# Quarters of the former unit's output product among the seven products of gate and up

## The chip, the cores and the metric

The kernel runs on one core of one Trainium2 chip. A core has five engines that run side by side: TensorE (PE in the profile; its weight loads have a row of their own, PEld), VectorE (DVE), ScalarE (ACT), GpSimd (POOL) and SyncE (SP, which issues most DMAs). The metric is the device time of one execution in microseconds (us). The time before is 747.75 us, the median of three runs (747.67, 747.75 and 748.01).

## The reference

Two transformer layers on x of shape 4 x 256 x 256 in float32, each with an attention of 16 heads and an FFN of 1024 hidden units, all with a layer norm ahead and a residual behind. The part that matters here is the FFN of the second layer:

```
up_gate = jnp.einsum('bsd,hd->bsh', x, W1)
up_lin = jnp.einsum('bsd,hd->bsh', x, W3)
hidden = jax.nn.silu(up_gate) * up_lin
hidden = fwht(hidden)
out = jnp.einsum('bsh,dh->bsd', hidden, W2)
```

## The kernel before

The kernel runs first attention, first FFN, second attention and second FFN in that order. The second FFN (`ffn1`) works in eight units, n = 0 to 7: unit n is one batch of 256 tokens (b = n // 2) and one half of the 1024 hidden units (half = n % 2). A unit has two parts.

The first part is `gated1`: the gate and up products of this batch with this half. Each is computed by a scheme with seven block products in place of eight (a Winograd form of Strassen's), written in `seven_products`. The seven run on TensorE in the order 5, 1, 2, 6, 3, 7, 4. Each product is four float32 matmuls of 128x128 by 128x128; the trace shows a float32 matmul as two records, so a product is eight records. The products go into three PSUM buffers, x (`gu_x`), y (`gu_y`) and z (`gu_z`). Product 5 goes to y; 1 to x; 2 to z; 6 is added to x; 3 is added to y; 7 is added to x; 4 is added to x. Because a sum is built up in a buffer from which partial values are taken, there are waits between the products:

- Product 6 may add to x only when ScalarE has copied x as product 1 left it (line 638).
- Product 7 may add to x only when ScalarE has copied x as product 6 left it (line 644).
- Product 4 may add to x only when VectorE has read x as product 7 left it (line 650, which forms the block c22 of the result).

Behind product 4, ScalarE copies x once more (line 653), then takes the silu of the gate half (line 852), and VectorE multiplies by the up half (line 853). The result is the tile h, the hidden values of the unit. In the last unit, n = 7, silu and multiplication are done in two halves of 128 tokens each, and the first half needs only products 5, 1, 2, 6 and 3.

The second part is `down`: the output product of unit n - 1. For each of two blocks of 128 tokens (t = 0, 1) it issues four float32 matmuls of 128x128 by 128x256 into a PSUM bank `po_f` (line 590). A batch's two units add up in the same two banks, and behind the second of them VectorE adds the residual (line 597) and SyncE stores 128 KB of output (line 600). The Walsh-Hadamard transform has been folded into the weights `w2h` before. A quarter of `down` is two float32 matmuls, four records; there are 16 records in all.

Two things set the order of the work. The code's order is: all of `gated1` of unit n, some norms and block sums for later batches (`normed`, `left_of`), then all of `down` of unit n - 1. The framework then plans each engine's order: it goes through the instructions with its own estimate of each duration, gives each engine the earliest instruction in the code's order that is ready by that estimate, and passes over one that is not ready yet. The engine then runs the planned order as it stands and waits where the estimate was wrong. So `down` may already be taken between two products of `gated1`, though it stands behind them in the code.

The first FFN uses the same `down` on lines 530 and 536.

Of the kernel before, what the change touches and what calls it, by code (L numbers as in the profile page):

```python
# [48 lines left out]
def two_layers(ctx, tc, consts, tables, x, wq, wkv, wo, w_gate, w_up, w_down,  # L49
# [26 lines left out]
    def bank(shape, name):  # L76
        return ps1.tile([P, *shape], F32, tag="bank", name=name)

    def page(name):

        return work.tile([P, 4, T], F32, tag="page", name=name, bufs=8)
# [24 lines left out]
    def load_ffn(src, shape, name):  # L106
        t = fpool.tile([P, *shape], F32, tag="fw", name=name)
        nc.sync.dma_start(t, src)
        return t
# [20 lines left out]
    down_sb = load_ffn(w_down, (NF, D), "w_down")  # L130
# [388 lines left out]
    def ffn0():  # L519
        hs, xn = {}, dict(enumerate(xn_f))  # L520
        for n in range(8):
            b, gc = divmod(n, 2)
            hs[n] = h = gated(xn[b], gate_sb, up_sb, 4 * gc, "h")
            a = page("a")
            nc.scalar.activation(a, h, AF.Abs)
            keep_two_of_four(a, h)
            if gc == 0 and b + 2 < B:
                xn[b + 2] = normed(b + 2, by_dma=True)
            if n >= 2:
                down(hs, n - 2, down_sb)  # L530
            if n == 4:
                xn1[0] = normed(0, by_dma=True)
            if n == 6:
                xn1[1] = normed(1, by_dma=True)
                left1[0] = left_of(xn1[0])
        return lambda: [down(hs, n, down_sb) for n in (6, 7)]

    def gated(xnT, w_g, w_u, f0, name):

        ps = []  # L540
        for w in (w_g, w_u):
            o = wide("pgu").rearrange("p two (f t) -> p (two f) t", t=T)
            for j in range(4):
                for c in range(NC):
                    nc.tensor.matmul(  # L545
                        o[:, j, :], lhsT=w[:, c, f0 + j, :], rhs=xnT[:, c, :],
                        start=(c == 0), stop=(c == NC - 1),
                    )
            ps.append(o)
        s, h = page("s"), page(name)  # L550
        nc.scalar.activation(s, ps[0], AF.Silu)
        nc.vector.tensor_tensor(h, ps[1], s, ALU.mult)
        return h

    def keep_two_of_four(a, h):

        c = []
        counts = work.tile([P, 8, T], BF16, tag="page", name="counts", bufs=8)  # L560
        for i in range(3):
            n = 3 - i
            ci = counts[:, (0, 3, 5)[i] : (3, 5, 6)[i], :]
            nc.vector.tensor_tensor(
                ci, a[:, i : i + 1, :].to_broadcast([P, n, T]), a[:, i + 1 :, :], ALU.is_ge
            )
            c.append({i + 1 + k: ci[:, k, :] for k in range(n)})
        sums = (
            (c[0][1], ALU.add, c[0][2], ALU.add, c[0][3], 2.0, ALU.is_ge),
            (c[1][2], ALU.add, c[1][3], ALU.subtract, c[0][1], 1.0, ALU.is_ge),  # L570
            (c[2][3], ALU.subtract, c[0][2], ALU.subtract, c[1][2], 0.0, ALU.is_ge),
            (c[0][3], ALU.add, c[1][3], ALU.add, c[2][3], 1.0, ALU.is_le),
        )
        for j, (u, op0, v, op1, w, bound, keep) in enumerate(sums):
            n = counts[:, 6 + j % 2, :]
            nc.vector.tensor_tensor(n, u, v, op0)
            nc.vector.tensor_tensor(n, n, w, op1)
            nc.vector.scalar_tensor_tensor(h[:, j, :], n, bound, h[:, j, :], keep, ALU.mult)
# [3 lines left out]
    def down(hs, n, w, last=False):  # L582


        b, gc = divmod(n, 2)
        if gc == 0:
            pos[b] = [bank([D], "po_f") for _ in range(NT)]
        for t in range(NT):
            for j in range(4):
                nc.tensor.matmul(  # L590
                    pos[b][t], lhsT=hs[n][:, j, t * P : (t + 1) * P],
                    rhs=w[:, 4 * gc + j, :], start=(gc == 0 and j == 0),
                    stop=(gc == 1 and j == 3),
                )
            if gc == 1:
                x = xs[b * NT + t]
                nc.vector.tensor_tensor(x, pos[b][t], x, ALU.add)
                if last:
                    at = (b * NT + t) * P
                    nc.sync.dma_start(out[at : at + P, :], x)  # L600

# [6 lines left out]
    def left_of(xnT):  # L610

        s = late.tile([P, 4, P], F32, tag="xs4", name="xs4", bufs=4)
        x11, x12, x21, x22 = (xnT[:, c, t * P : (t + 1) * P] for t in range(2) for c in range(2))
        for i, a, b, op in (
            (0, x21, x22, ALU.add), (1, s[:, 0], x11, ALU.subtract),
            (2, x11, x21, ALU.subtract), (3, x12, s[:, 1], ALU.subtract),
        ):
            nc.vector.tensor_tensor(s[:, i], a, b, op)
        return x11, x12, s[:, 3], x22, s[:, 0], s[:, 1], s[:, 2]
# [10 lines left out]
    def seven_products(product, x, z, y, c11, c12, c21, c22, shape, z_alone=True):  # L630


        u = [late.tile(shape, F32, tag="u", name="u", bufs=4) for _ in range(3)]
        product(y, 5, True)
        nc.scalar.copy(u[1], y)
        yield
        product(x, 1, True)
        nc.scalar.copy(u[0], x)
        yield
        product(z, 2, z_alone)  # L640
        nc.vector.tensor_tensor(c11, z, u[0], ALU.add)
        yield
        product(x, 6, False)
        nc.scalar.copy(u[2], x)
        yield
        product(y, 3, False)
        nc.vector.tensor_tensor(c12, y, u[2], ALU.add)
        yield
        product(x, 7, False)
        last_of["sum"] = nc.vector.tensor_tensor(c22, x, u[1], ALU.add)  # L650
        yield
        product(x, 4, False)
        last_of["copy"] = nc.scalar.copy(c21, x)  # L653
        yield
# [99 lines left out]
    def st(shape, name):  # L754
        return st_pool.tile(shape, F32, tag="st", name=name)
# [74 lines left out]
                              [t[:, i, k] for k in range(4)]))  # L830
        return r

    def gated1(x, r, last):


        def product(o, i, first):
            for j in range(4):
                nc.tensor.matmul(  # L838
                    o[:, j, :], lhsT=r[j // 2][i - 1][:, j % 2, :], rhs=x[i - 1],
                    start=(first and j == 0), stop=True, skip_group_check=True,  # L840
                )

        gu = late.tile([P, 2, 4, T], F32, tag="qk", name="gu")
        c = gu.rearrange("p k (a m) (t c) -> p (k a) m t c", m=2, t=NT)
        for _ in seven_products(
            product, st([P, 4, P], "gu_x"), bank([4, P], "gu_z"), st([P, 4, P], "gu_y"),
            *(c[:, :, m, t, :] for t in range(2) for m in range(2)), [P, 4, P],
        ):
            pass
        s, h = page("s"), page("h1")  # L850
        for t in (slice(0, P), slice(P, T)) if last else (slice(0, T),):
            nc.scalar.activation(s[:, :, t], gu[:, 0, :, t], AF.Silu)
            nc.vector.tensor_tensor(h[:, :, t], gu[:, 1, :, t], s[:, :, t], ALU.mult)
        return h

    def ffn1():
        hs, left = {}, {0: left_of(xn_f[0])}
        for n in range(9):
            if n < 8:
                b, half = divmod(n, 2)  # L860
                hs[n] = gated1(left[b], r_ffn1[half], n == 7)
                if n == 0:
                    xn = {1: normed(1)}
                if half == 1 and b + 2 < B:
                    xn[b + 2] = normed(b + 2, by_dma=True)
                if half == 0 and b + 1 < B:
                    left[b + 1] = left_of(xn[b + 1])
            if n >= 1:
                down(hs, n - 1, w2h[0], last=True)

    xn_f, xn1, left1, w2h, r_ffn1 = [], {}, {}, [], []
    attention0()
# [8 lines left out]
    load_group1(1)  # L881

    finish_ffn0 = ffn0()
    xn_f.clear()
    ps2_open.close()
# [3 lines left out]
    st_open, st_pool = open_pool("st", bufs=4, space=PSUM)  # L889
    attention1(finish_ffn0)  # L890
    ffn1()
    st_open.close()

# [81 lines left out]
```

## Time and profile before

| what | value |
|---|---|
| median of three runs | 747.75 us |
| the profiled execution's own time | 746.65 us |
| its span in the profile | 744.8 us |
| PE busy over the span | 734.0 us, 99% |
| PEld busy over the span | 599.4 us, 80% |
| DVE, ACT, POOL busy | 464.3, 405.8, 338.2 us |
| second FFN, first product to last output sum | 660.75 to 741.91 us |
| units 3 to 6, from start of product 5 to the next unit's | 9.98 to 9.99 us each |

The span is the time between the first and the last instruction of the profiled execution; 1.85 us of that execution lie around it. Busy times of the engines add up to far more than the span, since they run side by side. In the timeline a row is a run of equal instructions: its start, its duration, the engine, the line, the tile written and the tiles read, and in square brackets how long the engine was idle before it and what ended that.

### The profile page before, as it was taken

Reading aid. Unit: us, or ns where it says so; the run is one execution under the profiler, and the core shown is the slowest. Engines: PE = TensorE matmul, PEld = TensorE weight load, DVE = VectorE, ACT = ScalarE, POOL = GpSimd, SP = SyncE. Lnnn points to the kernel's source line nnn. Section 1 sums busy time; section 2 is a strip of 40 time slices with the busy share of each in tenths; the row PEclk is TensorE's granted clock in tenths of the full one; section 3 lists DMA queues with packets and bytes.
Section 4 is the critical chain, followed back from the end, with each engine's and each line's share of the span. In section 5 each row is a group of like instructions: output and inputs, shape, how many; then the busy total and the mean of one; then the engine's idle time right before and its main releaser. Section 6 shows DMA issues by size and latency. Waiting matters only on the chain.

```text
span 744.8 us, 11648 instructions
## 1 busy us (share of the span) xinstructions
PE 734.0 (99%) x3956; PEld 599.4 (80%) x3956; DVE 464.3 (62%) x1398; ACT 405.8 (54%) x985; POOL 338.2 (45%) x479
## 2 busy tenths in 40 slices
PE   8999999999999999999999999999999999999998
PEld 5556566666667678888898999999998999899997
DVE  6999877888887517986655644464443548355333
ACT  2487887677767932322355555555554775324432
POOL 1587978887899801011125433343335683210000
PEclk9999999999999999999999999999999999999999
DMA  8732254434444451002224433542232222000000
GB/s 329 284 64 55 53 99 84 80 63 89 84 81 89 85 189 53 15 15 62 81 71 96 118 43 43 113 87 44 44 72 44 44 44 43 0 3 20 22 15 29
DMA packets 127882, 54.87 MB, mean 74 GB/s; under 512 B 121040, under 2 KB 123216, under 8 KB 127056
## 3 DMA queue, kind: packets, MB, share of 16 engines
q1 hardware_dynamic: 127824, 54.15, 31.5%
q8 instruction: 31, 0.51, 0.3%
q14 instruction: 27, 0.22, 0.1%
HBM read 22.94 MB, written 1.05 MB: 32 GB/s over the span
## 4 chain that ended last, share of the span: by engine, by line
PE 87%; DVE 8%; ACT 3%; POOL 1%; issue 1%; ACTq 0%; DVEq 0%; POOLq 0%
PE pj L440 11%; PE po L282 7%; PE pgu L545 7%; PE qk_x L764 7%; PE po_f L590 7%; PE po L294 6%; PE sc L205 6%; PE gu_x L838 4%; PE av L270 4%; PE qk_y L764 3%; PE v_x L770 3%; PE av L388 3%; PE sc L204 3%; PE v_zy L770 3%; PE gu_y L838 2%; PE av L273 2%
## 5 line engine op out<-in xcount | busy, mean ns | idle before, releaser
L225 POOL TENSOR_SCALAR p<-p,rs 128x128 f32<-128x128 f32 (+1 forms) x256 | 115.4, 469 | 149.6 <-DVE rs L222 146.4
L242 POOL TENSOR_SCALAR pl<-p 128x1536 uint16<-128x1536 uint16 x58 | 87.8, 1513 | 4.0
L207 DVE CUSTOM_DVE_ANT_0 p<-sc,cst 128x128 f32<-128x128 f32 (+1 forms) x256 | 79.8, 352 | 11.0 <-PE sc L205 8.3
L262 ACT COPY pT<-plT 128x1536 uint16<-128x1536 uint16 (+1 forms) x58 | 84.0, 1509 | 0.0
L217 ACT ACTIVATE p<-p,nb,r 128x128 f32<-128x128 f32 (+1 forms) x128 | 68.2, 534 | 18.7 <-DVE nb L214 18.6
L440 PE MATMUL pj<-wq,xnT 128*128 128x512 f32 x128 | 61.2, 595 | 1.8 <-DVE qT L503 1.1
L440 PE MATMUL pj<-wkv,xnT 128*128 128x512 f32 x128 | 60.3, 592 | 0.0
L217 ACT ACTIVATE p<-p,nb 128x128 f32<-128x128 f32 (+1 forms) x128 | 56.3, 445 | 5.7 <-DVE nb L212 5.7
L294 PE MATMUL po<-wo,zT 128*128 128x256 f32 x256 | 57.8, 379 | 0.0
L282 PE MATMUL po<-w_o,zT 128*128 128x256 f32 x256 | 57.7, 379 | 0.0
L155 POOL TENSOR_SCALAR ve<-mv 128x2 f32<-128x2 f32 x16 | 3.5, 219 | 116.0 <-DVE mv L152 115.6
L450 ACT ACTIVATE sq<-pj 128x512 f32<-128x512 f32 x64 | 31.0, 491 | 43.0 <-DVE qc L445 42.7
L294 PEld LDWEIGHTS po<-wo,zT 128*128 128x128 f32 x256 | 48.3, 190 | 7.0 <-ACT kT L514 0.6
L282 PEld LDWEIGHTS po<-w_o,zT 128*128 128x128 f32 x256 | 47.5, 190 | 5.8
L440 PEld LDWEIGHTS pj<-wkv,xnT 128*128 128x128 f32 x128 | 24.3, 190 | 30.2 <-issue 28.7
L445 DVE TENSOR_TENSOR qs<-pj,sin_s 128x512 f32<-128x512 f32 x64 | 35.4, 552 | 13.7 <-PE pj L440 13.2
L440 PEld LDWEIGHTS pj<-wq,xnT 128*128 128x128 f32 x128 | 23.5, 190 | 24.9 <-issue 19.8
L653 ACT COPY qk<-qk_x 128x512 f32<-128x512 f32 x16 | 9.4, 586 | 57.6 <-PE qk_x L764 57.6
L270 PE MATMUL av<-pT,v 128*128 128x256 f32 x128 | 38.8, 385 | 0.9 <-ACT pT L262 0.7
L205 PE MATMUL sc<-kT,qT 128*128 128x256 f32 x128 | 38.3, 381 | 0.0
L205 PE MATMUL sc<-qk 128*128 128x256 f32 x128 | 38.2, 380 | 0.0
L484 POOL TENSOR_TENSOR r<-ve,mhalf 128x12 f32<-128x12 f32 x16 | 37.3, 2328 | 0.8
(154 smaller groups left out, 1750.8 us busy)
## 6 DMA issues: line engine op xcount, KB each, us to landing
w<-in_w_dram SPq DMA_DIRECT2D x3, 1024.0 KB, 4.8
wq<-in_wq_dram SPq DMA_DIRECT2D x4, 512.0 KB, 7.4
wkv<-in_wkv_dram SPq DMA_DIRECT2D x4, 512.0 KB, 7.9
wo<-in_wo_dram SPq DMA_DIRECT2D x4, 512.0 KB, 10.2
w_qk<-in_w_q_dram SPq DMA_DIRECT2D x4, 512.0 KB, 4.6
w_qk<-in_w_k_dram SPq DMA_DIRECT2D x4, 512.0 KB, 5.5
w_v<-in_w_v_dram SPq DMA_DIRECT2D x4, 512.0 KB, 6.7
w_o<-in_w_o_dram SPq DMA_DIRECT2D x4, 512.0 KB, 6.5
```

The costliest lines, as they stand in the source:

```text
L205: nc.tensor.matmul(sc[:, P : 3 * P], lhsT=q[:, P:T], rhs=k, start=True, stop=True)
L207: last_of["mx"] = nc.vector.tensor_tensor_reduce(out=p[:, j, cols], in0=sc[:, cols], in1=mask[:, cols], scale=1.0, scalar=-3.0e38, op0=ALU ...
L217: last_of["exp"] = nc.scalar.activation(p[:, j, cols], p[:, j, cols], AF.Exp, bias=nb[:, j, i : i + 1], scale=SCALE1 if rq is None else rq ...
L225: nc.gpsimd.tensor_scalar(p[:, j, cols], p[:, j, cols], rs[:, j, i : i + 1], 1.0, ALU.mult, ALU.mult)
L242: last_of["planes"] = nc.gpsimd.tensor_scalar(o, i, 1.0, 1.0, ALU.mult, ALU.mult)
L262: copy(words.rearrange("p (n w) -> p w n", w=2), halves[:, :, js].rearrange("p w j n -> p w (j n)"),)
L270: nc.tensor.matmul(av, lhsT=v0, rhs=pT[:, 0:T], start=True, stop=False, skip_group_check=True)
L282: nc.tensor.matmul(po[:, t, :], lhsT=zT[:, j, t * P : (t + 1) * P], rhs=w[:, j, :], start=(t == j == 0), stop=(j == 3), skip_group_check=True,
L294: nc.tensor.matmul(po, lhsT=zTs[hd // 4][:, hd % 4, t * P : (t + 1) * P], rhs=w[:, hd, :], start=(hd == 0), stop=(hd == n - 1),)
L440: last_of[0] = nc.tensor.matmul(pj, lhsT=xnT[:, c, cols], rhs=w[:, g, c, :], start=(c == 0), stop=(c == NC - 1),)
L545: nc.tensor.matmul(o[:, j, :], lhsT=w[:, c, f0 + j, :], rhs=xnT[:, c, :], start=(c == 0), stop=(c == NC - 1),)
L764: last_of[1] = nc.tensor.matmul(o[:, j, :], lhsT=wqk[i - 1][:, j // 2, j % 2, :], rhs=x[i - 1], start=(first and j == 0), stop=True, skip_ ...
```

## The change

`down` becomes a generator that pauses four times, once behind each quarter (two float32 matmuls). `gated1` takes such a generator, `between`, and draws from it: one quarter behind product 6 (the fourth in order), and two quarters behind product 7 (the sixth in order), ahead of product 4. In `ffn1` the generator is `down` of unit n - 1, and what is left of it, the fourth quarter, is issued behind `gated1`, ahead of the norms and block sums that stood ahead of `down` before. Unit 0 has no former unit and gets an empty iterator. `down` of unit 7 is issued whole, as before. The first FFN runs its generators to the end at once, so that its order in the code stays.

```diff
+                if j == 1:
+                    yield
             if gc == 1:
                 x = xs[b * NT + t]
                 nc.vector.tensor_tensor(x, pos[b][t], x, ALU.add)
                 if last:
                     at = (b * NT + t) * P
                     nc.sync.dma_start(out[at : at + P, :], x)
+            yield
+
+    def run(*generators):
+        for g in generators:
+            for _ in g:
+                pass
...
-        for _ in seven_products(
+        for i, _ in enumerate(seven_products(
             product, st([P, 4, P], "gu_x"), bank([4, P], "gu_z"), st([P, 4, P], "gu_y"),
             *(c[:, :, m, t, :] for t in range(2) for m in range(2)), [P, 4, P],
-        ):
-            pass
+        )):
+            for _ in range({3: 1, 5: 2}.get(i, 0)):
+                next(between, None)
...
-                hs[n] = gated1(left[b], r_ffn1[half], n == 7)
+                before = down(hs, n - 1, w2h[0], last=True) if n else iter(())
+                hs[n] = gated1(left[b], r_ffn1[half], n == 7, before)
+                run(before)
                 if n == 0:
                     xn = {1: normed(1)}
                 if half == 1 and b + 2 < B:
                     xn[b + 2] = normed(b + 2, by_dma=True)
                 if half == 0 and b + 1 < B:
                     left[b + 1] = left_of(xn[b + 1])
-            if n >= 1:
-                down(hs, n - 1, w2h[0], last=True)
+            else:
+                run(down(hs, n - 1, w2h[0], last=True))
```

In the first FFN, `down(hs, n - 2, down_sb)` becomes `run(down(hs, n - 2, down_sb))`, and the two that end it become `run(*(down(hs, n, down_sb) for n in (6, 7)))`.

More of the change, by code (lines that the diff above doesn't have):

```diff
@@ L529, in ffn0 @@
             if n >= 2:
-                down(hs, n - 2, down_sb)
+                run(down(hs, n - 2, down_sb))
             if n == 4:
@@ L535, in ffn0 @@
                 left1[0] = left_of(xn1[0])
-        return lambda: [down(hs, n, down_sb) for n in (6, 7)]
+        return lambda: run(*(down(hs, n, down_sb) for n in (6, 7)))
     def gated(xnT, w_g, w_u, f0, name):
@@ L831, in factors_ffn1, with gated1 @@
         return r
-    def gated1(x, r, last):
+    def gated1(x, r, last, between):
         def product(o, i, first):
```

## The prediction

> **What bounds the kernel now.** I read the page's busy times and slices first, then the stretch of the second FFN by units, then one unit in the timeline, the chain of work that ended last over the same unit, and the waits. The page:
>
> ```profile
> PE 734.0 (99%) x3956; PEld 599.4 (80%) x3956; DVE 464.3 (62%) x1398; ACT 405.8 (54%) x985; POOL 338.2 (45%) x479
> PEclk9999999999999999999999999999999999999999
> ```
>
> TensorE sets the time and its clock is full throughout, so a gain must be idle time of TensorE, and only in the second FFN, since the code's order changes nowhere else. One unit as a stretch (busy times of PE, PEld, DVE, ACT, POOL, then the clock):
>
> ```profile
> 707.88:717.86 9.98, 9.98 (x73) 9.30 (x72) 3.63 (x6) 3.40 (x5) 0.00 (x0) 1.00 0.06 20
> ```
>
> By the PE row there is nothing to gain: busy 9.98 of 9.98. But PE's ends are modelled and overlap (a product starts 0.89 after the last and is shown 1.06 long). The starts tell more. The same unit in the timeline:
>
> ```profile
> 708.77 1.06 PE L838 MATMUL gu_x<-xnT,w 128*128 128x128 f32 x8
> 709.66 1.06 PE L838 MATMUL gu_z<-xnT,w 128*128 128x128 f32 x8
> 710.50 0.97 PEld L838 LDWEIGHTS gu_x<-xs,t_gu 128*128 128x128 f32 x8
> 710.55 1.10 PE L838 MATMUL gu_x<-xs,t_gu 128*128 128x128 f32 x8
> 711.69 0.59 ACT L644 COPY u<-gu_x 128x512 f32<-128x512 f32 x1 [1.25 <-PE gu_x L838]
> 712.33 0.97 PEld L838 LDWEIGHTS gu_x<-xs,t_gu 128*128 128x128 f32 x8
> 713.53 0.69 DVE L650 TENSOR_TENSOR gu<-gu_x,u 128x512 f32<-128x512 f32 x1 [0.18 <-PE gu_x L838]
> 714.27 0.97 PEld L838 LDWEIGHTS gu_x<-xnT,t_gu 128*128 128x128 f32 x8 [0.32 <-DVE gu L650]
> 715.47 0.59 ACT L653 COPY gu<-gu_x 128x512 f32<-128x512 f32 x1 [3.19 <-PE gu_x L838]
> 716.09 1.06 ACT L852 ACTIVATE s<-gu 128x1024 f32<-128x1024 f32 x1
> 717.17 1.23 DVE L853 TENSOR_TENSOR h<-gu,s 128x1024 f32<-128x1024 f32 x1 [2.96 <-ACT s L852]
> ```
>
> And the chain over it (start, length):
>
> ```profile
> 710.72 0.94 PE gu_x L838 x8
> 711.66 0.89 PE gu_y L838 x8
> 712.55 0.94 PE gu_x L838 x8
> 713.49 0.87 PE po_f L590 x4
> 714.36 1.08 PE gu_x L838 x8
> 715.43 2.59 PE po_f L590 x12
> ```
>
> The reader should see two things. First, the plan already takes one quarter of the output product between products 7 and 4, and three behind product 4. Second, an undisturbed product takes 0.89 and a quarter 0.86 (2.59 / 3), but products 6 and 7 take 0.94 and product 4 takes 1.08. The extra is a late weight load: 0.05 before 6 (ScalarE's copy of x), 0.05 before 7 (its next copy), 0.19 before 4 (VectorE's sum). The waits over units 1 to 7 name the same releaser for the largest:
>
> ```profile
> PEld gu_x L838 <- DVE gu L650: 2.2, 7, 0.3
> ```
>
> Of each 0.32 idle on PEld, about 0.18 reaches the matmuls, because a quarter's loads are shorter than its matmuls.
>
> **The change part by part.** No instruction is added or taken away: the same 56 product records, 16 output records, sums, copies and stores. Only order changes, so every term is a stall that goes or comes. I write T for the start of product 4 in a unit.
>
> *Quarters 2 and 3 ahead of product 4.* From the start of product 7 to the load of product 4 is 714.27 - 712.39 = 1.88. Behind product 7 (0.89) now come two quarters (1.73), so the load would be wanted at 2.62 - 0.11 = 2.51 (0.11 is how far ahead an undisturbed load starts). The sum is then 0.63 early and the stall goes: -0.19 by the chain, -0.18 by single starts (297 and 213 ns, where 216 and 112 are normal). What is late next: nothing in this place until VectorE is 0.63 late; its extra work there, the block sums (line 618, four of 0.29), is less than twice that and falls elsewhere in the trace.
>
> *Quarter 1 between products 6 and 3.* From product 6 to the load of product 7 is 712.33 - 710.55 = 1.78; behind it now lie 0.94 + 0.86 + 0.89 = 2.69. The stall of product 7 goes: -0.05. This quarter waits for h of unit n - 1. In the unit shown h ends at 718.40, T + 4.13. Under the new order product 4 (0.89), the fourth quarter (0.86), products 5, 1 and 2 (0.89 each) and 6 (0.94) come first, so it is wanted at T + 5.27: 1.1 to spare. Behind it in TensorE's queue stand products 3, 7 and 4, and for these wait VectorE's sums and ScalarE's last copy, so a late h would move the whole unit.
>
> *Only the fourth quarter behind product 4.* Before, three quarters (2.59) covered ScalarE there; now 0.86 does. ScalarE needs: copy at T + 1.20, silu to T + 2.88, then the copy of product 5, which ends at T + 2.85 after its usual 1.09 from its start, so 2.90 to 3.49; the copy of product 1 starts at T + 3.74 as TensorE delivers it. That is 0.25 to spare, and product 6 keeps its 0.05 but gets no more. This is the cover that shrinks: if ScalarE comes more than 0.25 later, the excess goes straight into product 6.
>
> *Unit 1.* Its order is its own (products 3 and 5 of the next unit taken early, 0.25 lost at product 6, 0.07 at 7, 0.18 at 4), because ScalarE loads a table there (1.28). The plan's reasons there are not touched up to product 6, so I take only product 4's stall: -0.18.
>
> *The end.* In unit 7 two quarters fewer lie behind product 4. The last h half is ready at 737.41, T + 3.16. TensorE has before it product 4, a quarter and the first half of the last output product (1.73): its load is wanted at T + 3.38. It is 0.2 early: 0, but only because the first half needs just the first half of h, ready at 734.79.
>
> *The rest.* VectorE's residual sum for t = 0 (0.42) moves ahead of product 4's copy, behind the sum product 4 waits for: 0, with 0.63 spare. SyncE's store of t = 0 moves ahead likewise, past the two transposing DMAs of the norms at most; DMA share is 0.02 to 0.20 in these units and nothing on TensorE waits for a store: 0. Norms move behind the last quarter; their results are needed two units on: 0. The first FFN: same order, 0. A boundary between a product and a quarter costs -2 to +3 ns where nothing waits; two more per unit: 0.
>
> Sum: units 2 to 7, 6 x (0.18 + 0.05) = 1.38, and 0.18 for unit 1: -1.56. The profiled span goes from 744.8 to 743.2 and its execution from 746.65 to 745.1 (the 1.85 around the span stay). The median shown lies 1.1 above the profiled execution; taking the same gain from it, 747.75 - 1.56 = 746.2. Both ends for what the trace cannot show: at best all stalls of units 1 to 7 go, 2.1 by the same starts, 745.6; at worst of the small ones, below.
>
> [...] The row first: at boundaries where nothing waits (product 4 to a quarter, a quarter to product 5) the next group's load runs under the current matmuls and the starts stay 0.11 and 0.22 apart. [...]
>
> **The rivals.**
>
> *No new order:* the plan already interleaves, and may put the quarters as before. For it: quarter 1 sits before product 4 today. Against: the quarters now stand ahead in the code. 747.75. Chance 0.06.
>
> *The end opens:* if the last output product waits for the whole h, it starts at T + 3.21 and not T + 1.76: +1.45, leaving -0.1: 747.6. Against: silu of the first half (733.41) did start before product 7's sum ended (734.19), so parts are tracked. Chance 0.08.
>
> *ScalarE's turned copies* (line 186, two of 0.62 in two units) land before the copy of product 1. Each pair costs up to 1.25 - 0.25 = 1.0; one such unit gives 747.2, half a pair 746.6. Against: one pair ran behind the copy for product 7, one behind that for product 6; for it: the cover is thinner. Chance 0.08.
>
> *Exposed loads at the new boundaries:* 2 x 0.19 (a load's row) x 7 = 2.7, so 748.9. Chance 0.04.
>
> *Slower: h late for quarter 1.* If the plan puts silu (1.06) behind the copies of products 5 and 1 on ScalarE, silu starts at T + 4.36, h ends at T + 6.7, and quarter 1 waits 1.4 in each of units 2 to 7: +8.4 - 1.56, 754.6. It decides once h is later than T + 5.27. For it: the next copies are ready 1.7 earlier than before relative to silu. Against: silu starts 0.03 behind line 653's copy in every unit shown. With one copy in between, h ends at T + 4.8 and nothing is lost. Chance 0.10, with other orders that make quarter 1 wait.
>
> **How the numbers follow.** The forecast holds with 0.64, 745.9 to 746.5 by what the hundredths in the rows leave open. A measurement of this kernel tells about 0.2% (1.5 us) from no change, and 1.56 is just over it. So of the 0.64 I count 0.44 as faster and 0.20 as the same; the four middle rivals (0.26) are the same, the last is slower: 0.44, 0.46, 0.10. The range from 745.6 to 747.6 holds the forecast, the ScalarE rival and the end that opens, 0.80.
>
> **What the changed profile would show.** If right: in a unit four records of `po_f` between products 6 and 3, eight between 7 and 4, four behind 4; no idle time on PEld before product 4 by line 650; product 7 at 0.89, product 4 at 0.89, product 6 still 0.94; units 9.76 apart instead of 9.98; 28 output records at the end become 20 without a gap. Wrong if idle time appears on PEld before `po_f` released by line 853 (h late), before product 6 by line 638 (ScalarE late), or if the records come in the old order.

## The result and the profile after

The changed kernel takes 746.21 us (median of 20 runs, 745.69 to 746.65), the kernel before 747.73 us (median of 20 runs, 747.22 to 748.10). The ratio is 0.9979, 95% interval 0.9973 to 0.9986: 1.5 us faster, as forecast (746.2).

The chain of work that ended last, over unit 5 of the changed kernel from product 6 on (start, length). The helper's line 838 is 847 now:

```profile
710.92 0.94 PE gu_x L847 x8
711.86 0.87 PE po_f L590 x4
712.73 0.89 PE gu_y L847 x8
713.62 0.89 PE gu_x L847 x8
714.51 1.73 PE po_f L590 x8
716.24 0.89 PE gu_x L847 x8
717.13 0.87 PE po_f L590 x4
```

One quarter stands behind product 6, two behind product 7, one behind product 4. Product 7 went from 0.94 to 0.89 and product 4 from 1.08 to 0.89; product 6 kept its 0.94. The same as stretches of units 4 and 5 (span of the stretch, then busy PE, PEld, DVE, ACT, POOL, clock):

```profile
698.33:708.08 9.75, 9.75 (x73) 9.34 (x72) 4.34 (x9) 4.54 (x8) 0.00 (x0) 1.00 0.04 13
708.08:717.84 9.76, 9.76 (x74) 9.34 (x73) 3.73 (x5) 3.40 (x6) 0.00 (x0) 1.00 0.05 15
```

A unit takes 9.75 to 9.76 where it took 9.98. PE is still shown busy throughout; PEld, at nearly the same busy time (9.34 against 9.30), stands idle for 0.42 a unit where it was 0.68. The waits over units 1 to 7 name what is left on TensorE's weight loads:

```profile
PEld gu_x L847 <- ACT u L652: 0.2, 1, 0.2
PEld gu_x L847 <- ACT u L646: 0.2, 1, 0.2
```

The wait for VectorE's sum, 2.2 us over seven units before, is gone from the list. The two that remain are unit 1's.

The second FFN, from its first product to its last output sum, went from 81.16 us (660.75 to 741.91) to 79.59 (661.84 to 741.43): 1.57 less. Its first product and its last output sum in the changed kernel:

```profile
661.84 1.05 PE L847 MATMUL gu_y<-xs,t_gu 128*128 128x128 f32 x8
741.00 0.43 DVE L599 TENSOR_TENSOR x<-po_f,x 128x256 f32<-128x256 f32 x1 [1.30 <-PE po_f L590]
```

The spans of the two profiled executions differ by only 0.5 (744.8 and 744.3), because the second FFN began 1.09 later in the one of after. That came between 214 and 256 us, in the first attention, where the planned order of every engine is the same in both kernels. Two runs below that draw quarters inside the unit begin the second FFN as early as the kernel before (660.64 and 660.52), and one with the order of before begins it as late as the changed kernel (661.71). So the shift belongs to the execution and not to the change, and the lengths of the second FFN are the better measure of what follows. They are read from the traces to 0.01 us, while the three medians of the kernel before on record differ by up to 0.2.

### The profile page after: what moved, and what is told of

The parts are those of the page before. It is cut to its first block, busy times and chain, and to the rows that moved or that the text cites. A ratio compares the mean times of both kernels' runs of the same rounds, so it can differ in the third digit from the quotient of the medians.

```text
span 744.3 us, 11647 instructions
## 1 busy us (share of the span) xinstructions
PE 732.4 (98%) x3956; PEld 599.5 (81%) x3956; DVE 464.6 (62%) x1398; ACT 405.6 (54%) x985; POOL 334.7 (45%) x479
## 4 chain that ended last, share of the span: by engine, by line
PE 88%; DVE 7%; ACT 4%; issue 1%; POOL 0%; ACTq 0%; DVEq 0%; POOLq 0%
PE pj L440 12%; PE po L282 7%; PE pgu L545 7%; PE qk_x L772 7%; PE po_f L590 7%; PE po L294 7%; PE sc L205 6%; PE gu_x L847 4%; PE av L270 4%; PE qk_y L772 3%; PE v_x L778 3%; PE av L388 3%; PE sc L204 3%; PE v_zy L778 3%; PE gu_y L847 2%; PE av L273 2%
## 5 line engine op out<-in xcount | busy, mean ns | idle before, releaser
L242 POOL TENSOR_SCALAR pl<-p 128x1536 uint16<-128x1536 uint16 x58 | 85.3, 1472 | 4.4 <-POOL p L225 0.5
L242 POOL TENSOR_SCALAR qpl<-qc 128x1024 uint16<-128x1024 uint16 x20 | 28.8, 1450 | 19.0 <-PE av L392 8.3
```

Source lines behind the costliest of these rows:

```text
L242: last_of["planes"] = nc.gpsimd.tensor_scalar(o, i, 1.0, 1.0, ALU.mult, ALU.mult)
```

## The experiments

All run the whole computation; only order and grouping differ, and in one run a table is loaded early besides. Times are medians of 8 to 11 runs; each set has its own runs of the kernel before: 747.84 us for four of them on one chip (the changed kernel again, the two places alone, the single matmuls with the early table), 747.91 us for the other four on another.

**The changed kernel again.**

> The changed kernel unaltered, as the measure for the others on the same chip. Theory (stalls before products 7 and 4 are filled by quarters): 1.5 us below the kernel before, 746.2. Rival (the gain is a chance of layout or of the chip it ran on): anything between 0 and 1.5 below.

It took 746.20 us, ratio 0.9978 (0.9969 to 0.9987); its second FFN is 79.58 long. The gain comes back in a second set of runs. On the other chip the single matmuls without the table load (below), which hold the same covers, give 1.57 by the medians.

**One of the two places alone.** In `gated1`:

```diff
-            for _ in range({3: 1, 5: 2}.get(i, 0)):
+            for _ in range({3: 1}.get(i, 0)):
```

> Only the quarter behind product 6; the plan of the rest is left to the framework, which takes one quarter between products 7 and 4 in units 3 to 7 and a quarter and a half in unit 2. Theory: product 7 at 0.89 in units 2 to 7 (0.05 each), product 4 still at 1.08 except in unit 2: 0.3 + 0.18 = 0.5 us below the kernel before, 747.2. Rival (the quarters help by drawing VectorE's and SyncE's work forward, not by covering the sum ahead of product 4): at least half of the gain, 747.0 or less.

It took 747.53 us, ratio 0.9995 (0.9986 to 1.0004); its second FFN is 80.70 long, 0.46 less than before. From the chain, parts of unit 5:

```profile
712.36 0.86 PE po_f L590 x4
713.23 0.89 PE gu_y L847 x8
714.12 0.89 PE gu_x L847 x8
715.01 0.86 PE po_f L590 x4
715.88 1.08 PE gu_x L847 x8
```

Product 7 is at 0.89, product 4 still at 1.08 behind a single quarter. The 0.46 is what the theory gives, with the 0.18 of unit 2, where the plan itself put a quarter and a half behind product 7 and product 4 is at 0.89. The median's 0.31 agrees with it within what medians tell; by the interval alone the run can't be told from no change.

```diff
-            for _ in range({3: 1, 5: 2}.get(i, 0)):
+            for _ in range({5: 2}.get(i, 0)):
```

> Only the two quarters ahead of product 4, none behind product 6. The plan keeps two quarters there in units 2, 3, 5, 6 and 7, and splits them around product 7 in unit 4. Theory: product 4's stall (0.18) goes in five units and product 7's (0.05) in unit 4, product 7 stays at 0.94 in the other units: 5 x 0.18 + 0.05 = 0.96 us below the kernel before, 746.8. Rival (one place holds the whole gain): 746.2 as the changed kernel.

It took 746.96 us, ratio 0.9987 (0.9978 to 0.9996); its second FFN is 80.19 long, 0.97 less than before. From its chain, unit 6:

```profile
722.10 0.89 PE gu_y L847 x8
723.00 0.94 PE gu_x L847 x8
723.93 1.73 PE po_f L590 x8
725.66 0.89 PE gu_x L847 x8
```

Now product 4 is at 0.89 and product 7 at 0.94. Unit 4, where the plan put one of the quarters ahead of product 7, is the other way round (0.89 at product 7, 1.07 at product 4), and unit 1 keeps its stall at product 4 in both runs. Each place fills its own stall and no other. So the gain is neither one place's alone nor a matter of sums and stores that come earlier: those moved in both runs (in unit 6 the residual sum for t = 0 starts 0.11 and 0.20 behind product 4's start, where it was 2.06).

**All four quarters inside the unit.**

```diff
-            for _ in range({3: 1, 5: 2}.get(i, 0)):
+            for _ in range({2: 1, 3: 1, 5: 2}.get(i, 0)):
```

> All four quarters inside the unit: one more behind product 2, none left behind product 4. Theory (the fourth quarter covers ScalarE): with T the start of product 4, silu ends at T + 2.77, the copies of products 5 and 1 behind it end at T + 3.99, and product 6 wants to load at T + 3.46; it loses 0.59 instead of 0.05 in units 2 to 7, 3.2 us above the changed kernel, 749.4, with idle time before product 6's loads released by the copy of product 1. Rival (ScalarE had room, and only h sets how early a quarter may stand): product 6 undisturbed, a wait for h in front of the first quarter of at most 0.2 a unit, 746.0 to 747.4.

It took 748.38 us, ratio to the kernel before 1.0005 (0.9996 to 1.0014): the whole gain is lost and nothing on TensorE has become more work. The timeline of unit 4:

```profile
696.84 1.05 PE L847 MATMUL gu_x<-xnT,t_gu 128*128 128x128 f32 x8
697.73 1.06 PE L847 MATMUL gu_y<-xs,t_gu 128*128 128x128 f32 x8
698.54 1.06 ACT L862 ACTIVATE s<-gu 128x1024 f32<-128x1024 f32 x1
699.51 0.57 ACT L643 COPY u<-gu_y 128x512 f32<-128x512 f32 x1
699.97 0.59 ACT L646 COPY u<-gu_x 128x512 f32<-128x512 f32 x1
700.61 0.52 PEld L847 LDWEIGHTS gu_x<-xs,t_gu 128*128 128x128 f32 x4 [0.24 <-ACT u L646]
```

With nothing behind product 4, silu and two copies stand one behind the other on ScalarE, and product 6's load waits for the second. By starts (the distances from one start to the next, against those of an undisturbed group) product 6 loses 0.31 in each of units 3 to 7, where the changed kernel loses 0.05. So the fourth quarter does cover ScalarE. The size was wrong: 0.59 had been expected, because I laid the rows end to end. Silu is shown 1.06 long but the copy starts 0.97 behind it, and the copy, shown 0.57, is followed by the next after 0.46. A second loss had not been expected. At the end, the second half of the last output product waits for h:

```profile
737.79 1.89 PE L590 MATMUL po_f<-w_qkt,h 128*128 128x256 f32 x8
740.02 1.99 PE L590 MATMUL po_f<-w_qkt,h 128*128 128x256 f32 x8 [0.33 <-DVE h L863]
```

By starts this is 0.6. The second FFN is 81.84 long, 2.25 above the changed kernel, which agrees with the 2.2 between the medians of the two sets. Of it 1.3 is product 6 in units 3 to 7 and 0.6 the end; the other 0.3 fell in units 1 and 2, which the plan ordered differently. The rival's quarter in front of product 6 did not occur: the plan split product 6 and put the quarter in its middle.

**The end without halves of h.** The last unit's silu and multiplication on all 256 tokens at once, once on the changed kernel and once on the kernel before:

```diff
-                hs[n] = gated1(left[b], r_ffn1[half], n == 7, before)
+                hs[n] = gated1(left[b], r_ffn1[half], False, before)
```

```diff
-                hs[n] = gated1(left[b], r_ffn1[half], n == 7)
+                hs[n] = gated1(left[b], r_ffn1[half], False)
```

> The changed kernel, with silu and multiplication of unit 7 done on all 256 tokens at once. Theory (the end is covered only by the halves of h): h ends at T + 4.03, the last output product wants to load at T + 1.65 and starts at T + 4.09: 2.4 us above the changed kernel, 748.6, with an idle stretch of 2.4 on TensorE. Rival (the end has slack of its own, as two quarters fewer there cost nothing): 746.2 to 746.7.

> The kernel before, with the same whole h in unit 7. Theory: three quarters behind product 4 cover most of it; h ends at T + 4.13, the last output product wants to load at T + 3.48: 0.7 us above the kernel before, 748.4. So with a whole h the change would gain nothing: this run minus the run on the changed kernel with a whole h is -0.2. Rival: both rise by the same amount and the difference stays 1.5.

On the changed kernel it took 748.84 us, ratio 1.0018 (1.0009 to 1.0027); on the kernel before 748.29 us, ratio 1.0006 (0.9997 to 1.0016). The end of the changed kernel with a whole h:

```profile
735.16 1.03 PE L590 MATMUL po_f<-w_qkt,h 128*128 128x256 f32 x4
737.13 1.23 DVE L863 TENSOR_TENSOR h<-gu,s 128x1024 f32<-128x1024 f32 x1 [3.69 <-ACT s L862]
738.41 5.41 PE L590 MATMUL po_f<-w_qkt,h 128*128 128x256 f32 x16 [2.22 <-DVE h L863]
```

And on the kernel before:

```profile
739.44 3.72 PE L590 MATMUL po_f<-w_qkt,h 128*128 128x256 f32 x16 [0.49 <-DVE h L853]
```

By starts TensorE loses 2.38 + 0.10 in the first, and 0.66 + 0.10 in the second (2.4 and 0.7 expected). The difference is two quarters (1.73). The second FFN is 83.75 and 81.91 long; 1.7 of the 83.75 comes from a lowered clock, which the last section takes up. Without it the changed kernel is 0.15 longer (0.2 expected): with a whole h the gain of 1.5 is gone. So the quarters taken from behind product 4 had covered the end as well, and they could be spared only because half of h was ready. The medians differ by 0.55, but that is mostly the clock's doing: the five runs on the changed kernel with an undisturbed clock (748.14 to 748.52) have a median of 748.34, next to the 748.29 on the kernel before.

**Output matmuls drawn singly.** `down` pauses behind every matmul, and the draws are one, one and four:

```diff
-                if j == 1:
-                    yield
+                yield
...
-            yield
...
-            for _ in range({3: 1, 5: 2}.get(i, 0)):
+            for _ in range({2: 1, 3: 1, 5: 4}.get(i, 0)):
```

> Output matmuls drawn singly as one behind product 2, one behind product 6, four behind product 7 and two behind product 4, without the early table load. Theory: products 6, 7 and 4 undisturbed in units 3 to 7, unit 2 keeps product 6's 0.05, unit 1 as in the changed kernel: 5 x 0.05 = 0.25 us below the changed kernel, 746.0. Rival (product 6's 0.05 is a cost of the change of buffers): 746.2.

With it, the table of silu loaded early (in `prepare_ffn1`):

```diff
+            with tc.issue_after(last_of["exp"].ins):
+                nc.scalar.activation(
+                    small.tile([P, 12], F32, tag="warm", name="warm"), mhalf, AF.Silu
+                )
```

> Output matmuls drawn singly: one behind product 2, one behind product 6, four behind product 7, the last two behind product 4; and ScalarE loads the table of silu once ahead of the second FFN by a silu on a 12-column scratch tile. Theory: product 6 goes from 0.94 to 0.89 in units 2 to 7 (0.28 in all), unit 1 loses its 0.25 at product 6 and 0.07 at product 7: 0.6 us below the changed kernel, 745.6, units of 9.71. Rival (product 6's 0.05 is not ScalarE's copy but a cost of going from z to x): units stay at 9.75 and the time within 0.3 of the changed kernel, 745.9 to 746.2. Third: the table load delays a copy of the second attention and eats the gain.

Without the table load it took 746.34 us, ratio 0.9979 (0.9970 to 0.9988), with it 745.95 us, ratio 0.9973 (0.9963 to 0.9984). The second FFN is 79.61 and 79.33 long, against 79.58. From the chain of the run with the table load, unit 5:

```profile
709.46 0.89 PE gu_z L849 x8
710.36 0.43 PE po_f L590 x2
710.79 0.89 PE gu_x L849 x8
711.68 0.43 PE po_f L590 x2
```

Product 6 is at 0.89: one matmul of 0.43 in front of it is enough cover, and the 0.05 was ScalarE's copy, not a cost of going from one buffer to another. In both runs this holds in units 3 to 7. But each gave less than expected, and by their times alone both lie nearer the rival's values (746.2, and 745.9 to 746.2); it is the traces that decide for the theory. Without the table load, two single matmuls stand so early that they wait for h: by starts 0.10 in unit 1 and 0.15 in unit 2, which eats the 5 x 0.05. This is the timeline of unit 2:

```profile
681.00 1.22 DVE L861 TENSOR_TENSOR h<-gu,s 128x1024 f32<-128x1024 f32 x1 [3.20 <-ACT s L860]
682.28 0.70 PE L590 MATMUL po_f<-w_qkt,h 128*128 128x256 f32 x2
```

The load starts at 682.28, just behind h's end at 682.22. With the table load, unit 2 is clean as well, 6 x 0.05 is gained, but unit 1 still loses 0.35 (0.32 in the changed kernel) where 0 was expected:

```profile
669.93 1.07 ACT L864 ACTIVATE s<-gu 128x1024 f32<-128x1024 f32 x1
670.89 0.59 ACT L644 COPY u<-gu_x 128x512 f32<-128x512 f32 x1
671.53 0.74 PEld L849 LDWEIGHTS gu_x<-xs,t_gu 128*128 128x128 f32 x6
```

The table load, 1.28 long in the kernel before, is gone from here, yet silu of unit 0 itself still stands ahead of the copy that product 6 waits for: unit 0 has no former unit whose quarters could stand behind its product 4. Of the 0.35, 0.10 is a single matmul that waits for h. The third rival, a table load that delays the second attention, is out: from the 951st matmul record (at 255 us) to the second FFN the traces with and without the load both take 406.5 us. The intervals of this run's ratio and the changed kernel's overlap, but six of its eight runs lie below 746.07, the lowest of the eleven of the changed kernel in the same set, and the medians differ by the same 0.25 as the traces. What is left in its second FFN is 0.6, in units 0 and 1.

## Why the prediction was right

*The place of the gain.* Idle time of TensorE ahead of products 7 and 4 was read from starts and weight loads, against a PE row that showed no idle time. Measured, these stalls went and the other distances between starts stayed: 1.38 was reckoned for units 2 to 7 and 0.18 for unit 1, and the second FFN is 1.57 shorter. That the median meets the forecast to 0.01 is luck, as medians of one kernel differ by up to 0.2; the lengths are the closer test. The two runs with one place each show that the two covers are independent. The forecast of the profiled span, 743.2, was missed (744.3), by the 1.09 of the first attention that the change does not touch. The prediction held 0.2% to be barely told from no change; the interval of 20 runs, 0.9973 to 0.9986, tells it clearly.

*The order.* That the code's order would be taken over in units 2 to 7, and unit 1's differences kept up to product 6, was argued from the plan of before; the trace shows it. In unit 1 products 6 and 7 still take 1.14 and 0.97, as assumed; the reason given for that, the table that ScalarE loads, explains little of it: with the table loaded early unit 1 loses 0.35, against 0.45 in the run that differs from it only in the table. The rival of no new order is out.

*The cover behind product 4.* 0.25 was reckoned to spare on ScalarE. In the changed kernel's unit 5:

```profile
708.03 1.06 ACT L862 ACTIVATE s<-gu 128x1024 f32<-128x1024 f32 x1
709.17 0.58 ACT L643 COPY u<-gu_y 128x512 f32<-128x512 f32 x1
710.07 0.58 ACT L646 COPY u<-gu_x 128x512 f32<-128x512 f32 x1 [0.31 <-PE gu_x L847]
```

The copy of product 1 still waits for TensorE, for 0.31. The step was right, and its warning, that the excess beyond this goes straight into product 6, came true when the last quarter was taken away. Its size there was 0.31 a unit. The working had added the shown lengths of rows that overlap, so in the prediction, too, it erred to the safe side.

*The end.* 0.2 was reckoned to spare. In the changed kernel's timeline the second half of h ends at 738.65, and the half of the last output product that needs it begins 12 records of 0.216 behind 736.48, at 739.07, its load 0.11 before:

```profile
736.48 4.48 PE L590 MATMUL po_f<-w_qkt,h 128*128 128x256 f32 x20
737.96 0.69 DVE L863 TENSOR_TENSOR h<-gu,s 128x512 f32<-128x512 f32 x1 [2.58 <-ACT s L862]
```

That is 0.31 early, and no gap. The rival of an opening end had the mechanism right and its condition did not hold; with a whole h it cost 2.4.

*The other rivals.* The turned copies of ScalarE delayed no product 6: each of units 2 to 7 loses the same 0.05 there. No boundary showed an exposed load; quarters take 0.86 to 0.87 and products behind them 0.89. In the changed kernel's unit 5 the loads of the groups at the new boundaries start under the matmuls before, 0.11 and 0.22 ahead of the matmuls they are for: the first quarter's at 711.59 for 711.70, product 3's at 712.35 for 712.57. A late h in front of a quarter was seen only when the matmuls were drawn earlier, and then at 0.10 to 0.15 in one place of a unit, not the 1.4 of the rival. That rival has a slip in its working: with one copy in between, h is said to end at T + 4.8, with nothing lost. If that is the copy of product 5 (T + 2.85 to 3.44 by the same rows), silu and multiplication end at about T + 5.8, 0.5 behind the T + 5.27 that decides. In no run did a copy of the next unit stand ahead of silu in units 1 to 7, so this stayed untested.

## What to carry to other kernels

Where one engine is shown busy throughout, compare starts of equal groups with one another and look at the weight loads: here a group of 1.08 among groups of 0.89 was a stall with a releaser, VectorE's sum. Independent work placed ahead of each such wait was worth the stall here, with each piece longer than the shortfall (a quarter of 0.86 more in each place, against 0.05 and 0.19). But the piece is taken from another place; what it covered there, the next unit's copies and the last unit's tail, has to be reckoned as carefully, since here both had only 0.3 us to spare.

## What the runs showed that had not been expected

In one run the granted clock fell behind an idle stretch of TensorE. With the whole h on the changed kernel, TensorE stood still for 2.2 us, and the windows of that end show the granted clock in the column behind POOL:

```profile
736.00:738.00 2.00, 0.19 (x1) 0.00 (x0) 0.87 (x1) 1.06 (x1) 0.00 (x0) 1.00 0.00 0
738.00:740.00 2.00, 1.59 (x6) 1.34 (x7) 0.35 (x1) 0.00 (x0) 0.00 (x0) 0.82 0.00 0
740.00:742.00 2.00, 2.00 (x6) 1.57 (x5) 0.42 (x1) 0.00 (x0) 0.00 (x0) 0.50 0.00 0
742.00:744.00 2.00, 1.81 (x7) 1.23 (x5) 0.15 (x1) 0.00 (x0) 0.00 (x0) 0.83 0.19 66
```

By these windows the clock fell to 0.50 some 0.9 us behind the restart, for about 3.4 us (all 2.0 of the window from 740, and 0.7 of each window beside it), and output records that start 0.216 apart elsewhere started 0.427 apart, some 1.7 us in all. It did so in some executions and not in others: the mean granted clock is 0.997 or 0.998 in six of that kernel's eleven runs and 0.999 or 1.0 in five, and 3.4 us at half the clock lower the mean of a 747 us span by 0.002. The five take 748.14 to 748.52, the six 750.0 to 750.3, except for the profiled one at 748.84, whose second FFN began 1.3 earlier than the changed kernel's (660.52 against 661.84). In the profiled execution the fall came behind 2.2 us of idle time. That the idle time brought it about is the author's reading; what decides between the executions was not measured. In the run on the kernel before, with 0.7 us of idle time by starts at the same place, the output records stayed 0.216 apart, its runs lie in one group (747.98 to 749.01), and none has a mean clock below 0.999.
